# Feed-forward of a two-layer attention network: the order of the layer norm's first chunk, of a q copy and of the last k copy

## The chip, the cores and the metric

One core of one Trainium2 chip runs the whole network in one program. The metric is the device time of one execution in microseconds; the median of three runs is given, and one profiled execution stands beside it. TensorE is called PE here, VectorE DVE, ScalarE ACT, GpSimd POOL and SyncE SP, as in the profile.

## What is computed

The input is a batch of 8 images, 384 channels of 32x32 positions in fp32. Two layers follow each other.

```python
x = x + L0(group_norm(x))             # attention, 8 heads of 48, relative bias from a small MLP
t = tokens(x)                         # 1024 tokens of 384 channels for each image
t = t + L1_attention(layer_norm(t))   # 6 heads of 64; q and k are normalised over each head's 64
t = t + L1_ffn(layer_norm(t))         # 384 -> 1536 -> 384, weights replaced by their signs
```

The feed-forward scales its hidden and its last activations by the largest magnitude in each of five groups of the batch. A group is one image (8 // 5), and the images beyond the fifth stay zero, so only the first five images have a feed-forward at all.

## The kernel before

The kernel works image by image. Every tile has 128 partitions; the 384 channels are three chunks (`KC`) of 128, and the 1024 tokens lie in the free dimension, in two halves of 512, since a matmul writes 512 columns.

Layer 0 runs first for all images and leaves its result in DRAM. Layer 1 (`_layer1`, the function that the diff touches) then goes through the images. For image b it runs 24 units of attention (3 pairs of heads x 2 halves of queries x 4 blocks of keys; scores at L1322, weighting at L1371), and then, for the first five images, interleaves two things in one hand-written order: the output projection and the feed-forward of image b, and the projections of q, k and v of image b+1, which give PE work while the feed-forward waits for its statistics.

That interleaved part is the `else:` branch ahead of the end of `_layer1`. In order:

- `project_out` (L1435, L1440) adds the attention to the tokens; ACT squares each chunk, and DVE folds the sums (L1724, L1725).
- `project(0, 0)` is the projection of q for pair 0 of image b+1 (`project_qk`, L1178). In the middle of it `token_sums` (L1145 to L1155) gives the sums for the layer norm of image b, by way of ACT (`trf`), SP and DRAM.
- `layer_norm` issues the statistics on POOL (L1162 to L1168, L1457) and three DMAs on SP: L1460 writes scale and shift to DRAM, L1462 and L1463 read them back spread over all partitions, as `lc` (scale) and `ls` (shift), 512 KB each. It returns `parts`, a list of pairs (`un`, `lun`) that fills up as the passes are written, and `finish`, called `normal` by its caller, which writes the passes: for each chunk `scaled` (DVE, L1467), `shifted` (DVE, L1470, and an ACT cast into fp32r, L1471), and `low` (DVE, L1475), which keeps what the cast lost.
- `project(0, 1)`, `project(1, 0)`, the head sums of pair 0 (PE, L1207; ACT copy `hr`, L1212; SP, L1213), and `project(1, 1)`, whose own copy is held back until `normal()` has written its passes.
- `feed_forward_1`: 12 groups of products of 12 matmuls each. Each chunk's value enters as two operands, `un` and `lun` (L1521). The first three groups are taken chunk by chunk, so that the first chunk is enough to begin. ACT takes each group out (L1505), DVE finds its maximum (L1508).
- `project(2, 0)`, then the quantising factor (POOL, and DVE L1499 to L1501), then `Supply`: `gelu(k)` on ACT (L1552), `split(k)` on DVE, which makes the two operands `hy` (L1560) and `ly` (L1561) of chunk k. Between them stands `project(2, 1)`, whose copy is held back as `take`. `project_v` of the last block follows (L1259; its copy is on ACT, L1265).
- `feed_forward_2`: 12 chunks k into three accumulators `y2p` (L1572), with the head sums of pair 2 and other small steps of image b+1 between chunks.

A projection is taken out of PSUM by `take()`: a DVE copy into `qk` (L1186 for q, L1188 with a reordering for k), then an ACT square into `qsq` (L1194). `project_qk` does that at once and steps the planner `later`, unless it is called with `step=False`; then it returns `take` for the caller to place, and doesn't step. `later` is a list of works that fall due after so many steps.

Engines take their instructions in the order of the program. What each waits for follows from tiles and buffers. Two pools of buffers matter: PSUM has four buffers of two banks, given out in turn to `pq`, `ts`, `hs`, `y1p`, `pv`, `y2p`; a new user waits until the last reader of the user before is done, which for `pq` is the square. The pool `work` has sixteen buffers of 128x1024 fp32, from which `un`, `lun`, `qsq`, `y1`, `hy`, `ly`, `hr`, `rq`, `lc` and `ls` are taken.

Of the kernel before, what the change touches and what calls it, by code (L numbers as in the profile page):

```python
# [63 lines left out]
class _Later:  # L64
# [16 lines left out]
    def finish(self):  # L81
        while self.due:
            self.step()
# [947 lines left out]
def _layer1(tc, ins, x1, out, shared, start, before=None, check=None):  # L1031
# [4 lines left out]
    with ExitStack() as ctx:  # L1036
# [10 lines left out]
        later = _Later()  # L1047
# [3 lines left out]
        def wtile(name, shape=(P, N)):  # L1051
            return work.tile(list(shape), F32, tag="w", name=name)
# [4 lines left out]
        def load(b):  # L1057

            if b % 2 == 0:
                t = shared.image(f"bx{b}")  # L1060
            else:
                t = xp.tile([P, KC, N], F32, tag="x", name=f"bx{b}")
            nc.sync.dma_start(t, x1[b].rearrange("(k p) n -> p k n", p=P))
            return t
# [95 lines left out]
        def token_stats(name, c):  # L1160

            nc.gpsimd.tensor_scalar(c, c, 1.0 / C, 1.0, ALU.mult, ALU.mult)  # L1162
            mean, var = c[:, 0], c[:, 1]
            sq = small.tile([P, MT], F32, tag="tq", name="tq" + name)
            nc.gpsimd.tensor_mul(sq, mean, mean)
            nc.gpsimd.tensor_sub(var, var, sq)
            nc.gpsimd.tensor_scalar(var, var, 1e-5, 0.0, ALU.add, ALU.add)
            nc.gpsimd.tensor_tensor(var, var, rsqrt.to_broadcast([P, MT]), ALU.pow)  # L1168
# [282 lines left out]

        def layer_norm(b, xt, c):

            high = wide.tile([P, KC, N], F32R, tag="o", name=f"un{b}")
            parts = []
            token_stats(f"f{b}", c)
            nc.gpsimd.tensor_mul(c[:, 0], c[:, 0], c[:, 1])  # L1457
            r = dram.tile([2, N], F32, tag="lr", name=f"lr{b}")
            with nc.allow_non_contiguous_dma(reason="statistics"):
                nc.sync.dma_start(bass.AP(r.tensor, r.offset, [[MT, P], [N, 2], [1, MT]]), c)  # L1460
            shift, scale = wtile(f"ls{b}"), wtile(f"lc{b}")
            nc.sync.dma_start(scale, r[1].partition_broadcast(P))  # L1462
            nc.sync.dma_start(shift, r[0].partition_broadcast(P))  # L1463
            un = [wtile(f"un{b}_{k}") for k in range(KC)]

            def scaled(k):
                nc.vector.tensor_mul(un[k], xt[:, k], scale)  # L1467

            def shifted(k):
                nc.vector.tensor_sub(un[k], un[k], shift)  # L1470
                nc.scalar.copy(high[:, k], un[k])  # L1471

            def low(k):
                t = work.tile([P, N], F32R, tag="w", name=f"lun{b}_{k}")
                nc.vector.tensor_sub(t, un[k], high[:, k].bitcast(F32))  # L1475
                parts.append((high[:, k], t))

            def finish():
                scaled(0)
                shifted(0)  # L1480
                for k in range(1, KC):
                    scaled(k)
                    low(k - 1)
                    shifted(k)
                low(KC - 1)

            return parts, finish

        def largest(name, parts):

# [117 lines left out]
        def head_rows(b):  # L1608
            return dram.tile([NP1, 8, HALF], F32, tag="hs", name=f"hd{b}")
# [35 lines left out]
        xt = first  # L1645
# [13 lines left out]
        for b in range(B):  # L1659


            assert B // NG == 1
            ffn, more = b < NG, b + 1 < B
            oT = None
            if b == 1 and check is not None:
                for i, stage in enumerate(check(wtile)):
                    later.after(2 * i + 5, stage)
            held = []
            for i, u in enumerate(units):
                done = held.pop(0) if len(held) == LAG else None  # L1670
                held.append(
                    (u, scores(b, qk, kc, u, lambda: weigh(b, oT, *done) if done else None))
                )
                if done and done[0][1:] == (NH - 1, MT // 2 - 1):
                    divide(b, oT, done[0][0])
                later.step()
                if i == 3:
                    if behind is not None:
                        behind()
                        behind = None  # L1680
                    oT = wide.tile([P, KC, N], F32, tag="o", name=f"oT{b}")
                    ahead = load(b + 1) if more else None
                    if more:
                        *ahead_sums, stages = fold(f"a{b + 1}", ahead)
                        for at, stage in zip((13, 14, 15, 19, 20), stages):
                            later.after(at - i, stage)
            if not more:
                for done in held:
                    weigh_last(b, oT, done)
                divide(b, oT, NP1 - 1)  # L1690
                later.finish()
                project_out(b, oT, xt, lambda m: store(b, xt, m))
                break
            if not ffn:

                def last(i, b=b, oT=oT, held=held):
                    weigh_last(b, oT, held[i])
                    if i == 1:
                        divide(b, oT, NP1 - 1, (2, 4))

                nqk, nkc = attention_inputs(
                    b + 1, ahead, [lambda: last(0), lambda: last(1)], ahead_sums
                )
                behind = lambda b=b, oT=oT, xt=xt: project_out(
                    b, oT, xt, lambda m: store(b, xt, m)
                )
            else:
                nqk, sq, d, nkc = {}, {}, head_rows(b + 1), kc_tile(b + 1)

                def project(pair, s, step=True, middle=None):  # L1710
                    return project_qk(b + 1, pair, s, ahead, nqk, sq, step, middle)

                def normalise(pair, *steps):
                    normalise_qk(b + 1, pair, nqk, d, nkc, steps)

                for i in range(2):
                    project_v(b + 1, ahead, i)
                    weigh_last(b, oT, held[i])
                divide(b, oT, NP1 - 1, (1, 1))
                project_v(b + 1, ahead, 2)  # L1720
                fsq, fc = [], []
                project_out(b, oT, xt, lambda m: fsq.append(square(f"f{b}", xt, m)), later.step)
                two = wtile(f"two{b}")
                nc.vector.tensor_add(two, xt[:, 0], xt[:, 1])  # L1724
                nc.vector.tensor_add(fsq[0], fsq[0], fsq[1])  # L1725
                project(
                    0, 0,
                    middle=lambda: fc.append(
                        token_sums(f"f{b}", (xt[:, KC - 1], two), (fsq[KC - 1], fsq[0]))
                    ),  # L1730
                )
                un, normal = layer_norm(b, xt, fc[0])
                tk = token_sums(f"a{b + 1}", *ahead_sums)
                project(0, 1)
                project(1, 0)
                head_sums(b + 1, 0, sq, d)
                take = project(1, 1, step=False)
                normal()
                take()

                def between_1(m):
                    if m == 2:
                        normalise(0, 5, 2)
                    elif m == 4:
                        head_sums(b + 1, 1, sq, d)
                        normalise(1, 5, 3)

                y1, top = feed_forward_1(b, un, between_1)
                project(2, 0)
                quant_scale(top)  # L1750
                supply = Supply(b, y1, top)
                supply.gelu(0)
                supply.gelu(1)
                supply.split(0)
                take = project(2, 1, step=False)
                supply.split(1)
                supply.gelu(2)
                take()
                project_v(b + 1, ahead, MT // 2 - 1, copy=nc.scalar.copy)

                def between_2(k):
                    if k == 0:
                        head_sums(b + 1, 2, sq, d)
                        normalise(2, 6, 3)
                    elif k == 4:
                        token_stats(f"a{b + 1}", tk)
                    elif k > 4 and (k - 5) % 2 == 0:
                        scale_v(tk, (k - 5) // 2)

                feed_forward_2(b, supply, between_2, xt)  # L1770
            xt, qk, kc = ahead, nqk, nkc
# [74 lines left out]
```

## Time and profile before

| what | value |
|---|---|
| median of 3 runs | 3058.92 us (3056.34 to 3061.76) |
| profiled execution | 3058.54 us; its span on the core 3056.7 us |
| busy in the span | PE 3023.9 us, DVE 1771.8, ACT 1401.7, POOL 463.0 |
| granted PE clock | 0.998 |
| first feed-forward in the span | about 1600 to 1725 us; the next ones 227 us apart |
| one DVE pass over 128x1024 fp32 | 1.22 us, starts 1.14 us apart in a row |
| DVE copy of k with reordering (L1188) | 1.91 to 2.00 us |
| ACT square (L1194), cast (L1471), gelu (L1552) | 1.02, 1.05, 1.13 us |
| DMA issues of `lc` and `ls` on SP, first image | 1626.92 and 1627.35 us |

The page of a profile gives busy time by engine, the span in 40 slices, the DMA queues, the chain of work that ended last and the costliest groups of instructions. Beside the page, a trace can be asked for the waits of one engine (who waited for whom, in total, how often and the longest), for the chain that ended last in order of time, for a timeline (start, length, engine, line and operation, tiles, and in brackets the idle time before it with what ended it), and for busy time and DMA traffic in given stretches. Times are from the start of the span. The ends of matmuls are modelled, so PE at 99% isn't PE at its peak.

### The profile page before, as it was taken

To read this page: it belongs to the slowest core of one execution; us is meant where nothing else is said; L and a number is where in the kernel's file an instruction comes from. 1 tells how busy PE (TensorE), PEld (TensorE's weight loads), DVE (VectorE), ACT (ScalarE), POOL (GpSimd) and SP (SyncE) were. 2 spreads that over 40 slices of the span, in tenths; PEclk is the share of its full clock that TensorE was granted. 3 is DMA by queue.
4 is the path that set the end of the run, shared out by engine and by line. 5 is a ranking of instruction groups with operands and counts; after the bars stand their busy time and mean duration, and the time that the engine had idled before them with its cause. 6 is when DMAs were issued, how large, how long until landed. Compare 5 with 4: busy or idle time off the path is not lost.

```text
span 3056.7 us, 45678 instructions
## 1 busy us (share of the span) xinstructions
PE 3023.9 (99%) x18914; PEld 1595.5 (52%) x18914; DVE 1771.8 (58%) x1768; ACT 1401.7 (46%) x1768; POOL 463.0 (15%) x315
## 2 busy tenths in 40 slices
PE   8999999999999999999999999999999999999998
PEld 3455546455554646444545645645645645644443
DVE  3746647273655637355565765755765755755545
ACT  2634526252443616244453553553544543554544
POOL 0111102021110202123202202202202202211110
PEclk9999999999999999999999999999999999999999
DMA  7412020211202020222401101101101101102011
GB/s 178 118 26 83 19 82 23 71 30 26 76 22 79 23 85 17 50 74 60 117 23 30 50 23 30 50 23 30 50 22 30 50 22 30 50 16 71 16 51 44
DMA packets 102770, 150.49 MB, mean 49 GB/s; under 512 B 62260, under 2 KB 65828, under 8 KB 101784
## 3 DMA queue, kind: packets, MB, share of 16 engines
q1 hardware_dynamic: 99688, 147.41, 16.8%
q8 instruction: 152, 2.49, 0.3%
q14 instruction: 66, 0.54, 0.1%
q10 hardware_dynamic: 2864, 0.05, 0.1%
HBM read 111.05 MB, written 27.32 MB: 45 GB/s over the span
## 4 chain that ended last, share of the span: by engine, by line
PE 92%; DVE 3%; DMA 2%; ACT 1%; SPq 1%; issue 1%; ACTq 0%; DVEq 0%
PE o L552 15%; PE s L521 15%; PE s L1322 11%; PE o L1371 10%; PE pq L467 8%; PE pq L1178 7%; PE y2p L1572 5%; PE pp L616 4%; PE y1p L1521 4%; PE pp L1435 4%; PE pv L1259 4%; PE pv L495 4%; PE sum L1394 1%; DVE qk L1188 1%; PE hs L1207 1%
## 5 line engine op out<-in xcount | busy, mean ns | idle before, releaser
L536 ACT ACTIVATE e<-e 128x1024 f32<-128x1024 f32 x512 | 534.9, 1056 | 441.9 <-DVE e L532 425.3
L532 DVE TENSOR_TENSOR e<-s,grow 128x1024 f32<-128x1024 f32 x512 | 601.0, 1217 | 190.6 <-PE s L521 190.1
L521 PE MATMUL s<-qk 48*64 48x512 f32 x4096 | 605.8, 591 | 2.3 <-DVE e L532 2.2
L552 PE MATMUL o<-e,v 64*64 64x512 f32 x4096 | 603.4, 591 | 1.5 <-DVE e L532 1.5
L1333 ACT ACTIVATE e<-s,kc 128x512 f32<-128x512 f32 x768 | 463.3, 693 | 181.2 <-PE s L1322 164.5
L1322 PE MATMUL s<-qk,qk 64*64 64x512 f32 x3072 | 398.6, 592 | 0.6 <-DVE oT L1381 0.4
L1371 PE MATMUL o<-e,v 64*64 64x512 f32 x3072 | 395.5, 591 | 0.0
L521 PEld LDWEIGHTS s<-qk 48*64 48x64 f32 x4096 | 238.5, 132 | 226.6 <-issue 82.3
L552 PEld LDWEIGHTS o<-e,v 64*64 64x64 f32 x4096 | 257.9, 133 | 182.6 <-issue 80.9
L1348 DVE TENSOR_TENSOR t<-t,e 128x1024 f32<-128x1024 f32 x192 | 230.8, 1221 | 65.6 <-ACT e L1333 65.6
L1178 PE MATMUL pq<-bx,wqkv 128*128 128x512 f32 x576 | 255.4, 596 | 0.7 <-ACT tra L1150 0.7
L467 PE MATMUL pq<-xn,w 128*128 128x512 f32 x576 | 251.5, 597 | 0.0
L1322 PEld LDWEIGHTS s<-qk,qk 64*64 64x64 f32 x3072 | 148.7, 132 | 195.0 <-issue 116.2
L581 POOL TENSOR_TENSOR inv<-sums,over 128x16 f32<-128x16 f32 x32 | 92.7, 2898 | 1015.1 <-DMA sums<-sd 856.0
L1371 PEld LDWEIGHTS o<-e,v 64*64 64x64 f32 x3072 | 148.1, 133 | 180.7 <-issue 142.7
L467 PEld LDWEIGHTS pq<-xn,w 128*128 128x128 f32 x576 | 109.5, 191 | 142.7 <-issue 140.2
L1178 PEld LDWEIGHTS pq<-bx,wqkv 128*128 128x128 f32 x576 | 107.4, 190 | 145.3 <-issue 141.5
L1345 DVE TENSOR_TENSOR t<-e,e 128x1024 f32<-128x1024 f32 x96 | 114.1, 1224 | 62.7 <-ACT e L1333 62.7
L1194 ACT ACTIVATE qsq<-pq 128x1024 f32<-128x1024 f32 x48 | 49.1, 1023 | 215.4 <-DVE qk L1188 110.0
L1508 DVE TENSOR_REDUCE parts<-y 128x1 f32<-128x1024 f32 x75 | 90.0, 1217 | 94.9 <-ACT y L1505 94.4
L1228 POOL TENSOR_TENSOR hc<-hc,rsqrt 128x32 f32<-128x32 f32 x24 | 139.4, 5810 | 2.0
L477 DVE TENSOR_SCALAR qk<-pq,bqk 128x1024 f32<-128x1024 f32 x24 | 30.8, 1284 | 177.6 <-PE pq L467 177.6
(161 smaller groups left out, 3028.3 us busy)
## 6 DMA issues: line engine op xcount, KB each, us to landing
rb<-rd SPq DMA_DIRECT2D x112, 256.0 KB
xn<-in_x_dram SPq DMA_DIRECT2D x24, 512.0 KB
res<-in_x_dram SPq DMA_DIRECT2D x24, 512.0 KB
x<-res SPq DMA_DIRECT2D x24, 512.0 KB
bx<-x SPq DMA_DIRECT2D x8, 1536.0 KB
rq<-hi SPq DMA_DIRECT2D x48, 256.0 KB
out_dram<-bx SPq DMA_DIRECT2D x24, 512.0 KB
wide<-table SPq DMA_DIRECT2D x80, 114.2 KB
```

Of the source, the lines that this page charges most:

```text
L467: nc.tensor.matmul(pq[:, h], wqk[:, k, s, 2 * pair : 2 * pair + 2, :].rearrange("p h d -> p (h d)"), xn[:, k, ts(h, HALF)], start=(k == 0) ...
L521: nc.tensor.matmul(s[j][ts(c, QP), i], qk[pair][rows, 1, ts(4 * m2 + 2 * i + c, QP)], qk[pair][rows, 0, ts(h, HALF)], start=True, stop=True,)
L532: nc.vector.tensor_add(e.rearrange("p (i q) -> p i q", i=2), s[j], bass.AP(near.tensor, near.offset, [near.ap[0], [-QROWS * IW, 2], [1, HA ...
L536: nc.scalar.activation(e, e, AF.Exp)
L552: nc.tensor.matmul(po[ts(j, S0), r], v[keys, 2 * m2 + i, 2 * pair + j, :], es[j][keys, ts(i, HALF)], start=(m2 == 0 and i == 0), stop=(m2 ...
L1178: nc.tensor.matmul(pq[:, h], wqkv[:, k, s * C + pair * P : s * C + (pair + 1) * P], xt[:, k, ts(h, HALF)], start=(k == 0), stop=(k == KC - 1),
L1228: nc.gpsimd.tensor_tensor(c, c, rsqrt.to_broadcast(list(c.shape)), ALU.pow)
L1322: nc.tensor.matmul(s[j][ts(c, QP), i], qk[pair, 1][rows, ts(4 * m2 + 2 * i + c, QP)], qk[pair, 0][rows, ts(h, HALF)], start=True, stop=True,)
L1333: nc.scalar.activation(e[:, ts(i, HALF)], s[j][:, i], AF.Exp, scale=kc[:, pair, j, m : m + 1])
L1348: nc.vector.tensor_add(total[j], total[j], e)
L1371: nc.tensor.matmul(po[ts(j, D1), r], v[keys, 2 * m2 + i, at : at + D1], es[j][keys, ts(i, HALF)], start=(m2 == 0 and i == 0), stop=(m2 == ...
L1572: nc.tensor.matmul(py[m][:, h], w2[:, k, ts(m, P)], supply.parts[k][i][:, ts(h, HALF)], start=(k == 0 and i == 0), stop=(k == FC - 1 and i ...
```

## The change

Two places of the interleaved order are changed; no operation is added or taken away.

First, `layer_norm` returns one more function. `begin` writes the passes of the first chunk (`scaled(0)`, `shifted(0)` with its cast); `finish` writes the rest. The caller projects q of pair 1 without taking it out, calls `begin()`, then takes q out and steps the planner. So the two DVE passes stand ahead of q's DVE copy, and the cast ahead of q's square on ACT.

Second, k of pair 2 is taken out directly after its projection has been issued: ahead of `split(1)` on DVE and ahead of `gelu(2)` on ACT, where before it stood behind both.

```diff
         def layer_norm(b, xt, c):
...
-            def finish():
+            def begin():
                 scaled(0)
                 shifted(0)
+
+            def finish():
                 for k in range(1, KC):
                     scaled(k)
                     low(k - 1)
                     shifted(k)
                 low(KC - 1)
 
-            return parts, finish
+            return parts, begin, finish
...
-                un, normal = layer_norm(b, xt, fc[0])
+                un, begin, normal = layer_norm(b, xt, fc[0])
                 tk = token_sums(f"a{b + 1}", *ahead_sums)
                 project(0, 1)
-                project(1, 0)
+                take = project(1, 0, step=False)
+                begin()
+                take()
+                later.step()
                 head_sums(b + 1, 0, sq, d)
                 take = project(1, 1, step=False)
                 normal()
@@
                 supply.gelu(0)
                 supply.gelu(1)
                 supply.split(0)
-                take = project(2, 1, step=False)
+                project(2, 1, step=False)()
                 supply.split(1)
                 supply.gelu(2)
-                take()
                 project_v(b + 1, ahead, MT // 2 - 1, copy=nc.scalar.copy)
```

The order of the instructions on PE, POOL and SP is the same in both programs; on DVE and ACT only the moved ones change places.

## The prediction

> **What bounds the kernel now.** I read the page first, then the waits of the matmul engine, then the chain that ended last and the timeline around each of those waits.
>
> ```profile
> PE 3023.9 (99%) x18914; PEld 1595.5 (52%) x18914; DVE 1771.8 (58%) x1768; ACT 1401.7 (46%) x1768; POOL 463.0 (15%) x315
> PE   8999999999999999999999999999999999999998
> ```
>
> PE is never idle for a slice, so a change to DVE and ACT order can only pay where PE stands still. PE's waits over the feed-forward part (us in total, times, longest):
>
> ```profile
> PE y2p L1572 <- ACT qsq L1194: 4.0, 5, 0.8
> PE y1p L1521 <- ACT qsq L1194: 2.1, 5, 0.4
> PE y1p L1521 <- DVE lun L1475: 2.1, 5, 0.4
> PE s L1322 <- DVE oT L1381: 0.4, 1, 0.4
> ```
>
> The first three come five times each, once per image with a feed-forward, and stand where the change moves work. The chain that ended last leaves PE in the same places; in the first such image:
>
> ```profile
> 1621.62 10.51 PE pq L1178 x24
> ...
> 1632.16 0.10 DVE qk L1186
> ...
> 1643.84 1.23 DVE lun L1475
> 1645.06 1.93 DVE qk L1188
> ...
> 1647.06 1.03 ACT qsq L1194
> 1648.10 0.04 issue
> 1648.14 5.83 PE y1p L1521 x24
> ```
>
> From 1632.16 DVE works off q's copy, eight layer-norm passes, k's copy; the square follows on ACT, and then PE may use the PSUM buffer. PE's own timeline gives the stalls their true size (start, length, group of two matmuls):
>
> ```profile
> 1644.07 0.63 PE L1521 MATMUL y1p<-un,w 128*128 128x512 f32 x2
> 1645.12 0.73 PE L1521 MATMUL y1p<-lun,w 128*128 128x512 f32 x2 [0.42 <-DVE lun L1475]
> ...
> 1647.07 0.63 PE L1521 MATMUL y1p<-lun,w 128*128 128x512 f32 x2
> 1648.14 0.73 PE L1521 MATMUL y1p<-un,w 128*128 128x512 f32 x2 [0.43 <-ACT qsq L1194]
> ```
>
> Undisturbed groups start 0.464 us apart (1638.76 to 1641.08, five steps in 2.32). Here the steps are 1.05 and 1.07.
>
> **What the Trainium skill says.** "Perfetto Trace Analysis", Per-engine timelines: a matmul's reported end is computed, not observed, and ACT and DVE are strict FIFOs. The trace agrees: it calls 0.42 us idle where the starts show 0.59 missing, so I count starts. "PSUM — Partial Sum Buffer", PSUM bank collisions: two engines must not touch one bank at once; so the square of q or k comes after DVE's copy of the same buffer, as in every pair here (copy 1644.98 to 1646.98, square 1647.06). "DMA: Bandwidth & Descriptors", Anatomy of one DMA: some 2.0 us plus bytes over 436 GB/s (fitted for another issuing path); estimate for the scale row, 524 KB issued at 1626.92: landed at 1630.1; the shift row behind it 1631.3. The trace moves 169 GB/s x 3.2 us = 541 KB to 1630.12 and 360 x 1.4 = 504 KB to 1631.52, so the last bytes come at 1631.5. "ScalarE: Activation LUTs", What ACT_TABLE_LOAD costs: 1283 ns for a switch of function set; the trace has five loads of 1283 ns, all ahead of the first gelu, and none around the square that already stands between gelus at 1690.38. So moving a square among gelus costs no load.
>
> **Part one: scaled(0), shifted(0) and the cast of chunk 0 ahead of q's copy.** No instruction is added; two DVE passes (1.22 us) and one ACT cast (1.05) change places with one DVE copy (1.22) and one square (1.02). No DMA or POOL work is in the moved steps, and `later.step()` keeps its place. DVE is idle from 1628.92 (end of k's copy, pair 0) to 1632.16. The two passes now stand there, each with a DMA wait that before was long over, and q's copy is queued behind them.
>
> The scale row: I take 1630.2. The shift row: bounded by its last bytes at 1631.5 and by SP's issue at 1631.89, which waits for a small DMA behind it on the same queue; in the other four images that issue comes 4.90 to 5.06 us after the scale row's, against 4.97 here. I take 1631.7. Then scaled(0) runs 1630.2 to 1631.4, shifted(0) 1631.70 to 1632.92, q's copy starts 1.14 later (the spacing of DVE passes in this trace) at 1632.84: 0.68 later than before. On from there, at 1.14 a pass and 1.05 for each cast with 0.03 on either side: low(0) 1635.1, low(1) 1638.6, low(2) 1642.1, k's copy 1643.24 to 1645.2, its square 1645.3 to 1646.3. Before: 1636.89, 1640.36, 1643.84, 1644.98, end 1648.08. So all but q's copy is 1.74 us earlier (two passes worth 2.42 less 0.68).
>
> What PE needs: its first feed-forward group stays at 1637.90, set by the projection ahead of it. Its first step is 0.86, but lun(0) is not the reason: the same 0.3 to 0.4 extra appears at 1688.33, where both operands were ready 1.8 us before. Then at 0.464 a group the second lun is due at 1641.54 (now finished at 1639.8), the third at 1644.3 (1643.3), and group m=3, which waits for k's square, at 1646.6 (1646.3). All three stalls go: 0.10+0.11, 0.59+0.10, 0.61+0.10 (a restart costs about 0.10 on the step after it), 1.61 us an image. Cover that thins: the square has 0.25 us; from a shift row 0.25 later on, every further 0.1 costs 0.1. Bounds for this part: 0.9 (the square's stall stays) to 1.6. I take 1.6.
>
> Who else moves: q's square ends at 1635.2, long before y1p(1) needs its buffer (1639.2). hr(0) follows it 0.7 us later than before, and with it pair 0's statistics on SP and POOL (5.4 to 6.3 us in POOL's power): kc is issued by 1649.2 instead of 1648.5, and SP's next task comes at about 1654. Nothing.
>
> **Part two: k of pair 2 ahead of the second chunk's halves.** In the first image, with the order of before:
>
> ```profile
> 1690.02 0.63 PE L1572 MATMUL y2p<-ly,w 128*128 128x512 f32 x2
> 1691.45 0.72 PE L1572 MATMUL y2p<-hy,w 128*128 128x512 f32 x2 [0.79 <-ACT qsq L1194]
> ```
>
> A step of 1.43 instead of 0.464: 0.96 lost, and 0.10 on the next (1692.01). Now DVE goes from ly(0) (1685.31) to k's copy at 1686.45, until 1688.41; its projection had ended by 1684.9. ACT squares 1688.5 to 1689.5, 1.0 ahead of PE's need at 1690.49. Saved: 1.06 an image.
>
> What is late next? gelu(2) stands behind the square: done at 1690.5 instead of 1686.6, wanted by DVE not before 1692.4. The v copy behind it ends at 1691.3 and PE's head sums want its buffer at 1691.5: 0.2 of cover, else up to 0.2 lost. hy(1) runs 1688.3 to 1689.0. In the built program ly(1) now takes the buffer that hy(0) held, so it waits for PE's last group that reads hy(0), begun at 1690.49: ly(1) starts near 1691.2 (0.11 after a group's end, as hy(2) does in before) and ends 1692.5. Queued behind it on DVE are hy(2) and ly(2); PE waits for ly(1) only at 1693.0, after the head sums (1.0) and a group. Cover 0.5 us; without it PE would lose at most what ly(1) is late. Bounds: 0 (this wait takes the square's place) to 1.06. I take 1.06.
>
> **Sum.** (1.61 + 1.06) x 5 = 13.3 us; the starts of the other four images give the same stalls within 0.02. The later work hangs on PE or on what PE releases: in the attention after it no PE wait is above 0.4 us, so an earlier PE is an earlier end. The profiled execution took 3058.54 (span 3056.7 and 1.84 around it), 0.4 below the median of 3058.92: 3045.2 on its own scale, 3045.6 on the median's.
>
> **Rivals.** (1) Only part counts: the shift row lands late enough to keep the square's stall (gain 0.9 + 1.06, 9.8 us: 3049), or ly(1)'s wait eats part two (8.0 us: 3051). For: covers of 0.25 and 0.5. Against: the bounds above hold in five images. (2) The time is given back: PE's earlier work meets the DMA chains of the next attention (inverse, spread, multiply), where the last chain runs over DMA twice an image: 3058.5. For: 5% of the chain from 1590 to 1860 is DMA (3.3% `rb`, 1.5% `rd`). Against: those chains start from PE's own sums and move with it. The text's "no change" means within 0.2% (6.1 us), about what a measurement here can tell. (3) Slower: DVE's queue stands at shifted(0) for a late shift row, with q's copy and all of the chain behind it. Every microsecond after 1631.95 is a microsecond for PE; the saving of 2.67 is used up at 1634.6. At 1637, double the measured time from issue, it is 2.4 us an image, 3071. Against: the 1631.89 issue.
>
> **Chances.** Full gain 0.70; rival 1 0.16; rival 2 with anything within 6.1 us 0.09; rival 3 0.05. So faster by over 0.2% 0.86, the same 0.09, slower 0.05. The range takes in the full gain with the spread of the runs (2.7 us either way) and rival 1 to its end: 3042.5 to 3051.
>
> **What would show it.** Right: PE's three waits gone from the list, starts 0.464 apart from 1637.9 on; a DVE wait for the shift row with q's copy about 0.7 late; lun(2) about 1.7 earlier; a short DVE wait of ly(1) for y2p. Wrong: y1p still waiting for qsq, y2p waiting for ly, or q's copy over 1 us late; all stalls gone and the span unmoved would be rival 2.

## The result and the profile after

| | before | after |
|---|---|---|
| median of six runs each, us | 3058.84 (3056.34 to 3061.76) | 3046.32 (3045.55 to 3049.08) |
| profiled span, us | 3056.7 | 3044.7 |
| first y1p to last y2p group, each image, us | 85.97 in all five | 83.52, 83.73, 83.61, 83.51, 83.47 |
| last y2p group to the next image's first y1p, us | 141.89, then 140.97 three times | 142.63, then 140.97, 140.98, 140.98 |

The ratio is 0.9964, interval 0.9954 to 0.9974: 12.5 us (8.0 to 14.1) against the 13.3 of the forecast. The two last rows are read from PE's timeline and carry most of what follows; a group is two matmuls of the same operands, one line of the timeline. They cut the trace into the stretch that the change touches (first y1p group to last y2p group of an image) and the way between two such stretches. Three of four ways agree within 0.01. How far a stretch repeats is shown further down: in a second trace of each kernel, the means of five images are 85.97 again for before and 83.70 for after, while single images of after lie between 83.47 and 83.87. The totals of one kernel lie up to 5 us apart.

The busy line of the page after:

```profile
PE 3018.3 (99%) x18914; PEld 1598.8 (53%) x18914; DVE 1772.1 (58%) x1768; ACT 1401.9 (46%) x1768; POOL 465.1 (15%) x315
```

DVE and ACT did the same work (1771.8 and 1401.7 before). PE did too, though its busy time fell by 5.6 us: a part of each stall is hidden in the modelled ends of the matmuls and counts as busy (the prediction's example has 0.59 us missing and 0.42 listed as idle). All waits of PE in the second layer after the change:

```profile
PE pp L1435 <- DVE oT L1419: 2.4, 1, 2.4
...
PE s L1322 <- DVE oT L1381: 1.2, 2, 0.7
PE pq L1178 <- ACT tra L1150: 0.7, 1, 0.7
```

The y1p and y2p waits for `lun` and `qsq` are gone from the list. (In the second trace of this kernel, two y1p waits for `qsq` are listed, 0.6 us together.) The wait in the attention (`s` for `oT`) rose from 0.4 to 1.2. DVE has two waits of five times each that bear on the change:

```profile
DVE ly L1564 <- PE y2p L1575: 11.2, 5, 2.3
...
DVE un L1468 <- DMA lc<-lr: 9.4, 5, 2.0
```

The first was forecast; in before, DVE stood five times for PE's y2p too, one chunk later (`hy`, 12.4 us). The second is on the scale row, not, as forecast, on the shift row. DVE in the first image after:

```profile
1629.78 1.23 DVE L1468 TENSOR_TENSOR un<-bx,lc 128x1024 f32<-128x1024 f32 x1 [1.85 <-DMA lc<-lr]
1631.09 1.23 DVE L1471 TENSOR_TENSOR un<-un,ls 128x1024 f32<-128x1024 f32 x1
1632.23 1.22 DVE L1186 COPY qk<-pq 128x1024 f32<-128x1024 f32 x1
...
1641.45 1.23 DVE L1476 TENSOR_TENSOR lun<-un,un 128x1024 fp32r<-128x1024 f32 x1 [1.12 <-ACT un L1472]
1642.60 1.98 DVE L1188 COPY qk<-pq 128x1024 f32<-128x1024 f32 x1
```

The scale row's DMA was issued at 1625.90, so 3.88 us passed until `scaled(0)`; the shift row was there when asked for. PE around the fourth y1p group, where k's square is needed:

```profile
1644.71 0.63 PE L1524 MATMUL y1p<-un,w 128*128 128x512 f32 x2
1645.18 0.63 PE L1524 MATMUL y1p<-lun,w 128*128 128x512 f32 x2
1645.73 0.73 PE L1524 MATMUL y1p<-un,w 128*128 128x512 f32 x2
1646.31 0.63 PE L1524 MATMUL y1p<-lun,w 128*128 128x512 f32 x2
```

Steps are 0.47, 0.55 and 0.58 where 0.464 is undisturbed: 0.09 + 0.12 lost, with no wait noted. In the other images it is 0.31, 0.19, 0.08 and 0.04, each with 0.11 behind it, 1.23 us in all. Counting starts shows what the list of waits leaves out.

### The profile page after: what moved, and what is told of

Read it like the earlier page. It is cut to its first block, busy times and chain, and to the rows that moved or that the text cites. A ratio compares the mean times of both kernels' runs of the same rounds, so it can differ in the third digit from the quotient of the medians.

```text
span 3044.7 us, 45670 instructions
## 1 busy us (share of the span) xinstructions
PE 3018.3 (99%) x18914; PEld 1598.8 (53%) x18914; DVE 1772.1 (58%) x1768; ACT 1401.9 (46%) x1768; POOL 465.1 (15%) x315
## 4 chain that ended last, share of the span: by engine, by line
PE 96%; DMA 1%; DVE 1%; SPq 1%; issue 0%; ACT 0%; ACTq 0%; DVEq 0%
PE s L521 14%; PE o L552 14%; PE s L1322 11%; PE o L1371 11%; PE pq L1178 8%; PE pq L467 8%; PE y2p L1575 6%; PE y1p L1524 5%; PE pp L616 4%; PE pv L1259 4%; PE pp L1435 4%; PE pv L495 4%; PE sum L1394 1%; PE hs L1207 1%; SPq L391 1%; DMA wide<-table 0%
```

## The experiments

In this table, the stretch is the mean of the five images, and the last column the first way, between images 0 and 1. Each run stood beside runs of before on its chip, with medians of 3058.55, 3058.32 and 3058.56 us in the three groups of runs; gains and ratios below are to these.

| run | total, us (runs) | stretch, us | way 0 to 1, us |
|---|---|---|---|
| before; again | 3058.84 (6); 3058.40 (13) | 85.97; 85.97 | 141.89; 142.45 |
| after; again | 3046.32 (6); 3048.39 (7) | 83.57; 83.70 | 142.63; 142.44 |
| part one; again | 3055.13 (21); 3055.45 (13) | 84.70; 84.89 | 142.07; 142.29 |
| part two; again | 3054.13 (21); 3053.39 (21) | 84.92; 84.91 | 142.11; 142.44 |
| shifted(2) ahead of low(1) | 3045.71 (5) | 83.46 | 142.84 |
| shift row late | 3057.39 (13) | 85.71 | 141.69 |
| range check a step later | 3046.49 (5) | 83.71 | 141.92 |
| three edits together | 3045.23 (5) | 83.47 | 141.80 |

**Part one alone.** The changed kernel with the second place as before:

```diff
-                project(2, 1, step=False)()
+                take = project(2, 1, step=False)
                 supply.split(1)
                 supply.gelu(2)
+                take()
```

> Part one alone: the first chunk's passes stand ahead of q's copy, k of pair 2 stays behind the second chunk's halves as before. My theory (two separate savings that add): part one saves 1.61 us an image less the 0.25 us that still remain at PE's fourth group, so 1.36 x 5 = 6.8 us, 3052.0 us against 3058.8; PE's waits for lun and for the square ahead of y1p are gone, its wait of y2p for the square stands at 4.0 us in five waits as before. Rival A (the next attention gives back what comes earlier): under 4 us, and PE waits in the attention that the kernel before lacks. Rival B (the gain is part two's almost alone, q's delay of 1.07 us eating part one): under 2 us.

Measured: ratio 0.9990 (0.9983 to 0.9996), 3.4 us, half of what was expected; but the stretch is 1.27 us shorter an image, 6.3 in five, near the 6.8 expected. PE's waits in it:

```profile
PE y2p L1575 <- ACT qsq L1194: 4.0, 5, 0.8
...
PE y1p L1524 <- ACT qsq L1194: 0.3, 1, 0.3
```

The lun waits are gone, the square's at y1p shows once, and the y2p wait stands untouched. The total is where rival A had put it (under 4 us), but its sign in the trace is missing: PE's one wait in the attention is 0.22 us, where before has one of 0.36. Rival B falls by the stretch. The total stays odd.

**Part two alone.** The kernel before, with the same lines the other way round.

> Part two alone: the layer norm as before, k of pair 2 taken out ahead of the second chunk's halves. My theory: 1.06 us an image, 5.3 us in all, 3053.5 us against 3058.8; the y1p waits stand as before, the y2p wait for the square is gone. Rival (the new wait of the second low half takes the place of the square's): no gain, with PE waiting for ly. If both parts are independent, the two gains add up to what both together gave (12.5 us by the medians).

Measured: 0.9986 (0.9979 to 0.9992), 4.4 us. The stretch is 84.92 us, 1.05 shorter in every image, and PE's waits at y1p (2.1 and 2.1 us, five each) stand as before while none for `ly` or the square is left at y2p. The new wait didn't take the place of the old one. By stretches the parts give 1.27 and 1.05, together 2.32; both at once gave 2.40. They add up. By the medians they don't: 3.4 and 4.4 make 7.8 us, where both at once gave 12.5.

**The rest at the fourth group.** The changed kernel with

```diff
-                for k in range(1, KC):
-                    scaled(k)
-                    low(k - 1)
-                    shifted(k)
-                low(KC - 1)
+                scaled(1)
+                low(0)
+                shifted(1)
+                scaled(2)
+                shifted(2)
+                low(1)
+                low(2)
```

> Both parts, and shifted(2) written ahead of low(1), so that the third chunk's cast runs while DVE makes the second low half, and DVE doesn't stand idle 1.12 us ahead of low(2). My theory: k's copy comes 1.1 us earlier, the rest of the stall at PE's fourth group (0.09 to 0.31 + 0.11 an image, 1.23 us in all) goes, so 1.2 us below the changed kernel, 3045.1 us. Rival: the second low half, now one pass later, comes late for PE (due 0.1 us after it is done by my working): the same as the changed kernel or up to 1 us slower, with a PE wait for lun in its place.

Measured: 3045.71 us. DVE's 1.12 us of idling is gone and the fourth group comes on time in all images. But the second `lun` is late in its place: 0.23 us in image 0, 0.05 to 0.18 in the others. The stretches together are 0.5 us shorter than in the first trace of the changed kernel and 1.2 shorter than in its second, so their sum doesn't tell theory from rival. The starts do: the stall at the fourth group went, as the theory said, and a smaller one came at the second `lun`, as the rival said.

**The shift row late.** The changed kernel with the DMA of the shift row taken out of `layer_norm` and issued later:

```diff
-            nc.sync.dma_start(shift, r[0].partition_broadcast(P))
+            def shift_row():
+                nc.sync.dma_start(shift, r[0].partition_broadcast(P))
...
                 tk = token_sums(f"a{b + 1}", *ahead_sums)
+                shift_row()
```

> Both parts, but the DMA that brings the shift row is issued on SP behind the two small DMAs of the next image's statistics instead of ahead of them. This tests the price of a late row: with q's copy and the whole chain queued behind shifted(0) on DVE. From the trace of the changed kernel the second small DMA can be issued once the first has landed, some 3 us after its own issue, so the shift row is issued near 1630 and lands near 1633.5 in the first image, 2.4 us later than shifted(0) now starts. Theory of the prediction (a late row costs PE one to one, the cover being used up): 2.4 us an image, 12 us above the changed kernel, 3058 us, about the kernel before. Second statement of the theory: the scale row, alone in its transfer, lands 3.2 us after its issue instead of 3.85. Rival (PE has cover, as the projection of pair 1 and the head sums lie between): under 3 us above the changed kernel.

Measured: 3057.39 us, ratio to before 0.9997 (0.9989 to 1.0005): the change's gain is gone. DVE in the first image of this run:

```profile
1628.48 1.23 DVE L1467 TENSOR_TENSOR un<-bx,lc 128x1024 f32<-128x1024 f32 x1 [1.94 <-DMA lc<-lr]
1632.21 1.23 DVE L1470 TENSOR_TENSOR un<-un,ls 128x1024 f32<-128x1024 f32 x1 [2.50 <-DMA ls<-lr]
1633.35 1.22 DVE L1186 COPY qk<-pq 128x1024 f32<-128x1024 f32 x1
```

And PE:

```profile
1635.51 1.02 PE L1526 MATMUL y1p<-un,w 128*128 128x512 f32 x2
1636.89 0.72 PE L1526 MATMUL y1p<-lun,w 128*128 128x512 f32 x2 [0.37 <-DVE lun L1475]
...
1640.37 0.73 PE L1526 MATMUL y1p<-lun,w 128*128 128x512 f32 x2 [0.43 <-DVE lun L1475]
...
1643.85 0.73 PE L1526 MATMUL y1p<-lun,w 128*128 128x512 f32 x2 [0.43 <-DVE lun L1475]
...
1646.86 0.73 PE L1526 MATMUL y1p<-un,w 128*128 128x512 f32 x2 [0.43 <-ACT qsq L1194]
```

PE waits for all three low halves and for k's square. Measured from PE's first y1p group, `shifted(0)` starts 2.51, 2.24, 1.86, 2.13 and 1.96 us later than in the changed kernel; the stretches are 2.52, 2.21, 1.87, 2.12 and 1.97 longer. The rival of this run is out: the cover is used up, and a late row costs one to one, as the third rival of the prediction priced it.

The second statement failed. The scale row, now without the other 512 KB behind it, took 3.84, 3.64, 3.34, 3.76 and 3.74 us from issue to `scaled(0)` (mean 3.66), against 3.81 to 4.07 (mean 3.91) in the changed kernel. The shift row alone took 3.52 to 3.92. So a row needs most of the delay by itself; the second row goes with about 0.25 us of it. Bytes don't tell the landing even then: the profile has 165 GB/s over the 3.20 us from the issue in the first image, 528 KB, nearly the whole of the row (524) and the small write beside it (8), and yet the pass began 0.64 us after that.

**What seemed to be given back in image 1.** In the changed kernel the way from image 0 to 1 is 0.74 us longer than in before. In that attention alone five small stages of a check on layer 0's sums (L726 to L741) run on DVE, one of them ahead of an inverse that DMAs and scores wait for. The changed kernel with

```diff
-                    later.after(2 * i + 5, stage)
+                    later.after(2 * i + 6, stage)
```

> The changed kernel, with the five stages of the range check (small DVE passes over layer 0's sums, in the attention of image 1 only) one planner step later, so that its fourth stage (0.42 + 0.69 us on DVE) no longer stands right ahead of the inverse of pair 0's sums. Theory on what was given back: in image 1 the way from the last y2p group to the next feed-forward's first y1p group takes 142.63 us instead of 140.97 as in the other images, because the inverse, its three DMAs and the multiply with oT come 1.06 us late and scores wait for PSUM behind them. With the stage moved that way takes 141.0 to 141.6 us and the first of the two attention waits of PE (0.5 us) goes; 1 to 1.6 us below the changed kernel. Rival (the DMAs' own spread in that image is the cause, not the inverse): 142.3 us or more as now, and the same total.

DVE in the changed kernel:

```profile
1759.73 0.42 DVE L732 TENSOR_SCALAR good<-good 128x512 f32<-128x512 f32 x1
1760.19 0.69 DVE L734 TENSOR_REDUCE bad<-good 128x1 f32<-128x512 f32 x1
1760.79 0.24 DVE L1412 RECIPROCAL inv<-inv 128x16 f32<-128x16 f32 x1
...
1767.98 1.23 DVE L1419 TENSOR_TENSOR oT<-oT,rb 128x1024 f32<-128x1024 f32 x1 [2.96 <-DMA rb<-rd]
```

And with the stage a step later:

```profile
1760.95 0.24 DVE L1412 RECIPROCAL inv<-inv 128x16 f32<-128x16 f32 x1
...
1765.95 0.42 DVE L732 TENSOR_SCALAR good<-good 128x512 f32<-128x512 f32 x1
1766.48 0.69 DVE L734 TENSOR_REDUCE bad<-good 128x1 f32<-128x512 f32 x1
1768.24 1.22 DVE L1419 TENSOR_TENSOR oT<-oT,rb 128x1024 f32<-128x1024 f32 x1 [1.07 <-DMA rb<-rd]
```

From the last y2p group on (1720.42 and 1721.63) the inverse comes at 40.37 and 39.32, the multiply at 47.56 and 46.61. PE's first wait there is gone, the second (0.5 us) stays; the way is 141.92, between theory and rival. The total, 3046.49, is the changed kernel's within its scatter.

**Before and after once more.**

> The kernel before once more, for the size of what varies outside the changed part: the way to the first y1p group (1637.9 us in the first profile of before, 1635.2 to 1636.9 in the others) and the last twelve matmuls (5.42 us in the first profiles of before and of the changed kernel, 7.11 in the four experiments). Theory (part one's 3.4 us by the medians against 5.9 by the trace is such variation or a place outside the part, not the mechanism): the stretch from the first y1p to the last y2p group is 994.7 us again within 0.3, while start and end move by 1 to 3 us. Rival (the changed part itself varies by microseconds from run to run): it moves too.

> The changed kernel once more, on the same chip as the last: the stretch from the first y1p to the last y2p group 983.4 us within 0.5, of it 83.5 to 83.8 in each image's feed-forward, and 142 to 143 us between the first two feed-forwards if the giving back in image 1 belongs to the kernel, 141.9 as in before if it was chance. Total 12 us below before.

Measured: before 3058.40 us, with 995.2 us from the first y1p group of image 0 to the last y2p group of image 4 (994.7 in the first trace); after 3048.39 us, 9.9 us less where 12 was expected, ratio 0.9967 (0.9956 to 0.9978), 983.9 us (983.4). So that part is 11.3 us shorter in either pair. Within it, the five feed-forwards were 12.0 us shorter in the first pair and 11.35 in this one. The way from image 0 to 1 was now 142.45 in before and 142.44 in after. In before:

```profile
1775.46 2.05 PE L1322 MATMUL s<-qk,qk 64*64 64x512 f32 x16 [0.62 <-DVE oT L1381]
1804.81 1.62 PE L1322 MATMUL s<-qk,qk 64*64 64x512 f32 x12 [0.39 <-DVE oT L1381]
```

Both waits are there without the change. In before alone this way varies by 0.56 us, and in the second pair nothing is given back, so the 0.74 us of the first pair can't be laid to the change. Outside the part, the way to the first y1p group took 1637.7 us in this run of before and 1634.6 to 1637.9 over all; what follows the last y2p group took 424.1 and 424.4 us in the first traces, 424.8 to 427.1 in all later ones, up to 1.7 us of it in the last twelve matmuls (5.42 to 7.11 us for the same x12 at L1435).

**The parts once more.**

> Part one alone once more. Open: by the medians it gave 3.4 us, while its trace has the stretch from the first y1p to the last y2p group 5.9 to 6.4 us shorter than in the two traces of before, and its profiled execution was 2 us faster than its median. Theory (what lies outside the changed part varies between builds' runs by 2 us, and the 3.4 was low by that): 3052.5 us here, 6 us below before, and the stretch 988.8 us again. Rival (part one alone costs 2 to 3 us outside its stretch in most executions): 3055 us again, with a place in the trace outside that stretch that is longer than in before.

> Part two alone once more, beside it: theory 3053.3 us, 5.2 us below before, the stretch 989.6 us again, 84.9 in each image. Together with part one's the two should make the 11.3 us by which the stretch of the changed kernel is shorter, if the parts are independent.

Part two: 3053.39 us, 0.9985 (0.9978 to 0.9992), 5.2 us, stretch 84.91: as expected. Part one: 3055.45 us, 0.9992 (0.9984 to 1.0001), 3.1 us again. Its stretches are 84.73 to 85.05, so 5.4 us shorter in five; with part two's 5.3 that is 10.7, for the 11.3 of both in the second pair. So the 3.4 wasn't low by chance. In its two traces what follows the last y2p group takes 427.0 and 427.1 us (424.8 to 426.8 in the others since the first pair), with the last multiply's wait 3.3 and 3.5 us (2.3 to 3.1), and a place in image 2's attention is 0.22 us longer in both. That is about half a microsecond to one; the rest of some 2 us isn't in its traces.

**Three edits together.** The two edits above, and q's copy between the two dependent passes of the first chunk:

```diff
-            def begin():
+            def begin(middle):
                 scaled(0)
+                middle()
                 shifted(0)
...
-                begin()
-                take()
+                begin(take)
```

> Three edits on the changed kernel: shifted(2) ahead of low(1); q's copy between scaled(0) and shifted(0) instead of behind both, so that it fills the extra 0.17 us between the two dependent passes; and the range check one planner step later. Theory: k's copy comes 1.3 us earlier than in the changed kernel, the rest at the fourth group (0.2 to 0.4 us an image) goes without the lun stall of up to 0.23 us that shifted(2) ahead of low(1) alone brought: y1p to last y2p 83.3 us in every image (83.5 to 83.7 in the changed kernel), 1.2 us in all; with the check's 1 to 1.6 us some 2.5 us below the changed kernel, 3043.5 us. Rival: the end of that stretch is set by PE alone already, so only the check's part comes, or neither.

Measured: 3045.23 us, ratio to before 0.9957 (0.9944 to 0.9971); on the same chip the changed kernel took 3048.39, with intervals that overlap. In the trace the stretches are 83.46 to 83.48 in all five images, not quite the 83.3 of the theory; in sum they are 417.4 us, for 417.9 and 418.5 in the two traces of after. In the first image 0.05 + 0.10 us at the second `lun` is all that is left. What is new is that the images agree: the scale row still took 3.80 to 4.18 us from its issue, but q's copy started 5.74 us ahead of the first y1p group in every image, as in before, where it started 4.32 to 4.72 ahead in after. The row's spread no longer reaches PE. It is the best version tried; that it beats the changed kernel is seen in the starts, not settled by the totals.

## Why the prediction was right, step by step

**Part one, forecast 1.61 us an image.** Three stalls were to go, two went whole: `lun` twice, 0.21 and 0.69. Of the third, k's square, 0.15 to 0.41 an image stayed (0.25 on average). One step of the working failed, the landing: the scale row was taken at 3.3 us from its issue, and the wait looked for on the shift row. Measured, the scale row came after 3.88, `shifted(0)` followed 1.31 later instead of 1.50 behind a late shift row, and q's copy started 6.33 us after the issue instead of 5.92. That is 0.41 later; the cover of 0.25 was used up and the rest showed at the fourth group (0.21 with the restart). The prediction had read the landing from bytes moved, 541 KB within 3.2 us. That count doesn't part the scale row from the shift row, issued 0.43 us behind it, and bytes moved are not yet a wait released.

The price of lateness was right, and the spread of the row shows it image by image. In the two traces of after, q's copy started between 4.72 and 4.32 us ahead of the first y1p group, and the stall at the fourth group grew with it: 0.04 us at 4.72, 0.19 at 4.58, 0.28 at 4.48, 0.46 at 4.32. The working had the copy 5.06 ahead, with 0.25 us of cover.

Size: with the restarts, the fourth group lost 0.25 and 0.39 us an image in the two traces of after, 0.32 and 0.50 in the two of part one alone. 1.61 less these makes 1.36, 1.22, 1.29 and 1.11. Measured were 1.35 and 1.22 (part two's 84.92 less the 83.57 and 83.70 of both), 1.27 and 1.08.

The prediction's own sign of failure, q's copy over 1 us late, came true by the letter (the projection ended at 1631.12, the copy started at 1632.23), and yet cost only that quarter of a microsecond. The limit was set too low: the chain behind the copy had two passes less to do. The sign "y1p still waiting for qsq" came true in small as well, in the starts and in the list of the second trace.

**Part two, forecast 1.06 us an image.** Measured 1.05. In the first image after:

```profile
1686.02 1.03 ACT L1194 ACTIVATE qsq<-pq 128x1024 f32<-128x1024 f32 x1 [2.83 <-DVE qk L1188]
1688.09 0.63 PE L1575 MATMUL y2p<-hy,w 128*128 128x512 f32 x2
1688.56 0.64 PE L1575 MATMUL y2p<-ly,w 128*128 128x512 f32 x2
```

The square ended at 1687.05, 1.04 us ahead of the y2p group that needs its buffer (1688.09), where 1.0 was forecast; the group after it starts 0.47 later, so no stall is left. DVE in the same image:

```profile
1685.83 0.67 DVE L1563 TENSOR_SCALAR hy<-y 128x1024 fp32r<-128x1024 f32 x1
1688.76 1.23 DVE L1564 SCALAR_TENSOR_TENSOR ly<-y,hy 128x1024 fp32r<-128x1024 f32 x1 [2.25 <-PE y2p L1575]
```

The wait of `ly(1)` for the buffer of `hy(0)` is there. It ended at 1689.99, 0.69 us before the group that reads it (1690.68), where 0.5 was forecast. The v copy ended at 1688.77, the head sums began at 1689.12: 0.35 for 0.2. One reading of this part was short: the trace of before has twelve table loads of 1.28 us on ACT, not five; five stand ahead of the first gelu of an image, and none around the square among the gelus, which is what the working rested on. The trace of after has twelve too.

**Sum, forecast 13.3 us.** 12.0 in the five feed-forwards of the first pair (2.67 less 0.25, five times, is 12.1), 11.35 in the second; 11.3 with the ways between them in both pairs; 12.5 and 9.9 by the medians. The 12.5 of the result is thus nearer to the forecast than the changed part earns; some 1 us of it is luck of the totals.

**Rivals.** The first (only part counts) happened in small: a quarter of a microsecond an image for the square, not 0.7, and nothing for `ly(1)`. The second (given back in the attention) didn't: the ways between the later feed-forwards are equal to 0.01 us, and the first varies by 0.56 us in before alone. The third was priced rightly at one to one, and the late row of the experiment paid it; in the changed kernel no pass was held up by the shift row: `shifted(0)` started 1.29 to 1.35 us after `scaled(0)`.

**Open.** Why part one alone is some 2 us slower by its totals than its stretches say, so that the parts add up by stretches and not by medians; and 1 us or more of scatter outside the changed part in every total.

## What to carry to other kernels

Compare traces by stretches between fixed instructions of the bounding engine, and take two traces of each kernel: here the mean of five stretches repeated within 0.2 us, where the totals of one kernel differ by 3 to 5. Where a pass is moved ahead to the moment when its data lands, take the landing from a wait that ended on it, with its spread, not from the bytes moved. Putting a pass that is ready between it and the pass that depends on it kept the spread away from PE here (tried only together with two other edits). Beside the waits that the profile lists for an engine, count the starts: 1.2 us were lost here with no wait shown.

## What the runs showed that had not been expected

A row of 512 KB spread over 128 partitions took 3.34 to 3.92 us from its issue to the pass that waits for it, when no second such row was issued with it, and 3.77 to 4.23 us in the seven traces with part one where the second row followed 0.43 us later. The page "DMA: Bandwidth & Descriptors" of the Trainium skill (Anatomy of one DMA) has a fit for another issuing path, from which the prediction's estimate of 3.2 us came; the measured times are longer and vary by half a microsecond and more. A pass that reads what the pass before it on DVE wrote started 1.31 us after it (1629.78 to 1631.09), an independent one 1.14.
